# A two-layer graph attention kernel: a new order table, ScalarE writes the last outputs first, x is added by accumulating transfers

## The chip, the cores and the metric

One core of a Trainium2 chip. The metric is the device time of one execution in microseconds (us). TensorE is called PE (matmul) and PEld (its weight loads), VectorE DVE, ScalarE ACT, GpSimd POOL and SyncE SP. SP and POOL issue the transfers (DMA).

## The reference

For each of 32 graphs of 512 nodes, with x of 512 numbers a node and an adjacency matrix of integers, all in float32: a layer norm and relu, two attention layers over the graph's edges, and x added at the end.

```python
def gat_layer(x, mask, W, a_src, a_dst, bias, concat):
    xl = (x @ W).reshape(B, N, H, F)
    asrc = jnp.einsum('bnhf,hf->bnh', xl, a_src)
    adst = jnp.einsum('bnhf,hf->bnh', xl, a_dst)
    e = jax.nn.leaky_relu(asrc[:, :, None, :] + adst[:, None, :, :], NEG_SLOPE)
    e = jnp.where(mask[..., None], e, NEG_INF)
    attn = jax.nn.softmax(e, axis=1)
    out = jnp.einsum('bsdh,bshf->bdhf', attn, xl)
    ...
h = jnp.maximum(_layernorm(x, axis=-1), 0.0)
h = jax.nn.elu(gat_layer(h, mask, W1, ..., concat=True))      # 4 heads of 256
x = x + gat_layer(h, mask, W2, ..., concat=False)             # 1 head of 512
```

## The kernel before, in words

Each graph goes through the same steps: `norm` (statistics on DVE, a power on POOL, the relu on ACT), `project1` (x times W1 for two pairs of heads), a softmax for each head, `gather1` (attention times projected nodes, with bias and ELU), `project2`, the softmax of the second layer, and `gather2`, which adds x and stores. Products are split into halves and done by seven products instead of eight (`sevens`); in `project1` the fifth of the seven is split once more into seven small ones of 128x129, the function `step`. A small product goes into one half of a bank `top` (keys tk+0 and tk+1) or straight into a result bank; ACT copies the result of the first, fourth and fifth out of `top` (the fifth into a buffer f), and DVE adds the sixth and seventh.

A softmax tile p of 128x512 per source block is made on DVE (`L517 ... p<-rr,z`, from normalisers rr that are spread over the partitions by a small store to DRAM and a load back, drr and rr on SP), gets the mask added by an accumulating transfer from DRAM that POOL issues (`p<-dm`, L525, two per pair of blocks), and goes through exp on ACT (`p<-p,z`). DVE sums p tiles into tiles t and hs for the seven products; PE multiplies them with xl.

`gather2` writes its result through `put`: for each of its seven products and two row blocks a result bank is scaled by the softmax share and added by DVE onto a tile t, which `residual` has loaded with x before (SP, 256 KB); when a tile t is complete SP stores it.

Nothing is emitted where it is written. Every instruction group is a job of the class `Program` (engine, cost, what it reads and writes), and `order()` decides the order in which jobs are emitted, and with it the order on each engine. Before, it is a list scheduling: a simulated clock with the costs and a model of the transfers (KIND), the job with the lowest rank first among those that are ready. The rank is a number of the table PLACES, one for each job of the start, of one turn, and of the end; the turn's numbers are used again for each graph, moved on by the turn's PE time. A turn has 470 jobs and works on the projection, the softmax and the gathers of neighbouring graphs side by side. Each engine runs its instructions in order, and waits for semaphores of others.

In the profile every operation of a helper has one line: L531 PE, L514 ACT, L517 DVE, L520 the transfers of SP, L525 those of POOL, L770 the power. Banks of PSUM are called mm, the weights w_sb, normalised and transposed x ht, sums of halves hs, hx (of activations) and wx (of weights, for the small products).

Of the kernel before, what the change touches and what calls it, by code (L numbers as in the profile page):

```python
# [19 lines left out]
P = 128  # L20
EPS = 1e-5
# [23 lines left out]
class Banks(Slots):  # L45
# [1664 lines left out]
```

## Time and profile before

| | us |
|---|---|
| time, median of 3 runs | 2773.44 |
| lowest, highest run | 2768.58, 2775.35 |
| the profiled execution | 2769.33 |
| its span | 2767.6 |

The rows of the profile that the prediction shows are read thus. A row of a timeline has the start and the length in us, the engine, the line, the operation, what is written and read, the shape, the count of instructions put together, and in brackets the time for which the engine stood before it and what ended that. A row of groups has the count, the busy time and the mean in ns of one, and the idle time before. A row of waits has who waited for whom: total, times, longest. Of an issue row the last number is the median time to landing.

### The profile page before, as it was taken

The numbers are of one execution on the slowest core, as the hardware profiler recorded it, in microseconds if no ns is written. First come the engines' busy times: TensorE is split into PE (matmuls) and PEld (weight loads), VectorE is DVE, ScalarE is ACT, GpSimd is POOL, SyncE is SP. The second block draws the span as 40 slices with busy tenths as digits, with TensorE's granted clock in tenths as the row PEclk, the third lists the DMA queues.
The fourth block names the chain that finished last, engine by engine and source line by source line (L and its number), as shares of the span: only waits on it lengthen the run. The fifth ranks groups of instructions, "written<-read, shape, count | busy, mean of one in ns | idle before, by whom it ended". The sixth has DMA issues, their size and how long they took to land. (4 is left out here: it accounts for less than half of the span.)

```text
span 2767.6 us, 42320 instructions
## 1 busy us (share of the span) xinstructions
PE 2742.4 (99%) x12924; PEld 2371.8 (86%) x12924; DVE 2558.2 (92%) x6732; ACT 2229.1 (81%) x4907; POOL 313.1 (11%) x356
## 2 busy tenths in 40 slices
PE   7999999999999999999999999999999999999999
PEld 6788888888888888888888888888888888888887
DVE  8999999999999999999999999999999999999996
ACT  5978888778887788877888877888778788788883
POOL 0110111101111111111011111111111111101110
PEclk9999999999999999999999999999999999999999
DMA  8657766667666667667676766766676767767563
GB/s 232 176 157 182 203 167 184 187 176 194 182 183 179 182 176 196 178 175 195 173 201 172 182 187 178 192 186 180 180 188 175 201 167 180 195 165 208 162 171 112
DMA packets 375864, 502.14 MB, mean 181 GB/s; under 512 B 222804, under 2 KB 227668, under 8 KB 375636
## 3 DMA queue, kind: packets, MB, share of 16 engines
q1 hardware_dynamic: 329844, 332.68, 42.4%
q0 software_dynamic: 45792, 166.74, 25.1%
q8 instruction: 103, 1.69, 0.3%
q14 instruction: 125, 1.02, 0.1%
HBM read 316.41 MB, written 51.31 MB: 133 GB/s over the span
## 5 line engine op out<-in xcount | busy, mean ns | idle before, releaser
L531 PE MATMUL mm<-w_sb,hs 128*128 128x257 f32 (+3 forms) x2908 | 667.0, 367 | 5.1 <-ACT mm L514 3.3
L531 PEld LDWEIGHTS mm<-w_sb,hs 128*128 128x128 f32 x2908 | 539.7, 190 | 87.7 <-ACT mm L514 6.7
L525 POOL DMA_DIRECT2D p<-dm x314 | 273.2, 875 | 2295.0 <-DVE p L517 764.3
L531 PE MATMUL mm<-w_sb,ht 128*128 128x258 f32 x2112 | 528.6, 382 | 2.7 <-ACT mm L514 2.5
L531 PE MATMUL mm<-p,xl 128*128 128x258 f32 (+1 forms) x1984 | 495.8, 383 | 0.1
L531 PE MATMUL mm<-w_sb,h 128*128 128x257 f32 x2056 | 477.8, 379 | 0.0
L517 DVE SCALAR_TENSOR_TENSOR p<-rr,z 128x512 f32<-128x512 f32 (+1 forms) x636 | 456.0, 742 | 2.4 <-DMA rr<-drr 2.4
L531 PEld LDWEIGHTS mm<-w_sb,ht 128*128 128x128 f32 x2112 | 393.7, 190 | 63.6 <-ACT mm L514 6.4
L514 ACT ACTIVATE p<-p,z 128x512 f32<-128x512 f32 (+1 forms) x636 | 433.4, 720 | 17.7 <-DVE p L517 12.4
L531 PEld LDWEIGHTS mm<-w_sb,h 128*128 128x128 f32 x2056 | 389.0, 189 | 58.4 <-ACT xl L514 0.5
L531 PEld LDWEIGHTS mm<-p,xl 128*128 128x128 f32 x1984 | 367.2, 190 | 52.7 <-issue 6.0
L514 ACT ACTIVATE mm<-mm 128x257 f32<-128x257 f32 (+2 forms) x498 | 169.8, 347 | 269.2 <-PE mm L531 236.2
L514 ACT ACTIVATE l<-as,z 128x512 f32<-128x512 f32 x516 | 354.4, 716 | 30.8 <-DMA as<-das 30.7
L514 ACT ACTIVATE l<-l,low 128x512 f32<-128x512 f32 x516 | 370.3, 721 | 7.6 <-DVE low L517 6.7
L517 DVE CUSTOM_DVE_ANT_1 l<-l,mt 128x512 f32<-128x512 f32 x516 | 346.2, 681 | 28.4 <-ACT l L514 27.4
L514 ACT ACTIVATE xl<-mm 128x258 f32<-128x258 f32 (+2 forms) x748 | 269.3, 382 | 91.4 <-PE mm L531 89.8
L514 ACT ACTIVATE h<-mm,b_sb 128x256 f32<-128x256 f32 (+1 forms) x504 | 231.0, 480 | 77.3 <-PE mm L531 76.6
L531 PE MATMUL mm<-t,hs 128*128 128x258 f32 (+1 forms) x992 | 246.1, 380 | 0.0
L517 DVE TENSOR_TENSOR xl<-xl,mm 128x258 f32<-128x258 f32 x372 | 155.3, 419 | 57.9 <-PE mm L531 48.3
L531 PEld LDWEIGHTS mm<-t,hs 128*128 128x128 f32 x992 | 185.8, 190 | 25.5 <-DVE t L517 0.2
L531 PE MATMUL mm<-xl,p 128*128 128x258 f32 (+2 forms) x752 | 189.7, 388 | 1.0 <-ACT h L514 0.6
L517 DVE SCALAR_TENSOR_TENSOR h<-xr,h 128x512 f32<-128x512 f32 x256 | 172.2, 683 | 6.1 <-ACT xr L514 6.1
(137 smaller groups left out, 3706.2 us busy)
## 6 DMA issues: line engine op xcount, KB each, us to landing
p<-dm POOLq DMA_DIRECT2D x314, 512.0 KB, 5.0
rr<-drr SPq DMA_DIRECT2D x159, 512.0 KB
x<-in_x_dram SPq DMA_DIRECT2D x129, 256.0 KB
adj<-in_adj_dram SPq DMA_DIRECT2D x128, 256.0 KB
as<-das SPq DMA_DIRECT2D x64, 512.0 KB
t<-in_x_dram SPq DMA_DIRECT2D x124, 256.0 KB
out_dram<-t SPq DMA_DIRECT2D x124, 256.0 KB
dm<-m SPq DMA_DIRECT2D x64, 256.0 KB
```

Source lines behind the costliest of these rows:

```text
L514: prog.add("ACT", cost, reads, writes, lambda: nc.scalar.activation(*a, **k))
L517: prog.add("DVE", cost, reads, writes, lambda: f(*a, **k))
L525: lambda: nc.gpsimd.dma_start(to, at, accum_op=OP.add), size,
L531: f(*a, **k)
```

## The change

Seven edits; the costs of jobs are no times, only what the order is made from.

1. `order()` is replaced. Each engine's jobs are sorted by rank (a new PLACES, in ten-thousandths of a microsecond instead of hundredths); the five lists are then merged by the lowest rank whose inputs have been emitted. The simulated clock and the model of transfers go. The order is so the same in each turn.
2. A small product that goes into `top` is listed as writing both halves of it, so that the next one comes behind the copy of the one before.
3. In `put` of `gather2`, products 2, 5, 6 and 4 are written to t by ACT as scaled copies, and only 3 and 7 are added by DVE: in each turn 8 of 12 adds become copies.
4. `residual` loads x only for the last graph. For the others POOL issues an accumulating transfer of x onto the finished t, 256 KB, four in a turn, and the store waits for its landing.
5. The norm of the first graph goes by tiles: four powers and shifts instead of one.
6. The identity for the first transposes lies in the buffer hx of the small products, and those transposes are listed as reading it.
7. The loads of the start come in another order, by the new table.

```diff
     def order(self):
...
+        lines = {e: [] for e in self.ENGINES}
+        for j in sorted(range(len(jobs)), key=lambda j: (rank[j], j)):
+            lines[jobs[j][0]].append(j)
+        lines = [deque(q) for q in lines.values()]
+        while any(lines):
+            q = min((q for q in lines if q and not left[q[0]]), key=lambda q: rank[q[0]])
+            j = q.popleft()
             done.append(j)
...
-        every = [sk + (t,) for t in range(NT)]
...
+        for ts in ([t] for t in range(NT)) if b == 0 else [range(NT)]:
+            every = [sk + (t,) for t in ts]
...
-                akeys + bkeys + ([tk + (1,)] if q == 1 else []), [bk], w / 576,
+                akeys + bkeys, [tk + (0,), tk + (1,)] if bk[:2] == tk else [bk], w / 576,
...
-            dma(XLOAD, [x2_key(b, 0, 0)], halves, xr, x[b, d * P : (d + 1) * P, :])
+            if b == B - 1:
+                dma(XLOAD, [x2_key(b, 0, 0)], halves, xr, x[b, d * P : (d + 1) * P, :])
+            else:
+                for c in range(2):
+                    prog.alias(xk + (c,), [xk, xk + (c,)])
...
-            dve(
-                PUT, [bk, sk, xk + (c,)], [xk + (c,)], nc.vector.scalar_tensor_tensor,
-                to, ps[:, :M], share, to, op0=OP.mult, op1=OP.add,
+            if n in (3, 7):
+                dve(
+                    PUT, [bk, sk, xk + (c,)], [xk + (c,)], nc.vector.scalar_tensor_tensor,
+                    to, ps[:, :M], share, to, op0=OP.mult, op1=OP.add,
+                )
+            else:
+                act(COPY, [bk, sk, xk], [xk + (c,)], to, ps[:, :M], AF.Copy, scale=share)
...
+                halves = [xk, xk + (0,), xk + (1,)]
+                accumulate(XADD, halves, halves, xt, x[b, d * P : (d + 1) * P, :])
                 dma(STORE, [xk, xk + (0,), xk + (1,)], (), out[b, d * P : (d + 1) * P, :], xt)
```

What the new order does at three places. First ACT in a turn, at the small products of the first pair of heads: `mm<-mm 128x129` is the copy of the first small product, `f<-mm` that of the fifth, `p<-p,z` are the exps. Before:

```order
L514 ACTIVATE mm_137<-mm_139 128x258
L514 ACTIVATE p_103<-p_103,z_127 128x512 x2
L514 ACTIVATE h_82<-mm_134,b_sb 128x256
L514 ACTIVATE xr_96<-h_82 128x512
L514 ACTIVATE p_103<-p_103,z_127 128x512 x2
L514 ACTIVATE mm_135<-mm_132 128x129
L514 ACTIVATE f_92<-mm_132 128x129
```

And of the change:

```order
L469 ACTIVATE mm_136<-mm_138 128x258
L469 ACTIVATE p_102<-p_102,z_126 128x512 x2
L469 ACTIVATE f_91<-mm_131 128x129
L469 ACTIVATE h_75<-mm_132,b_sb 128x256
L469 ACTIVATE p_102<-p_102,z_126 128x512
L469 ACTIVATE mm_134<-mm_131 128x129
L469 ACTIVATE xl<-mm_138 128x258
L469 ACTIVATE p_102<-p_102,z_126 128x512
```

Both copies stood behind four exps; now f stands behind two and the other behind three.

On PE at the same place (each matmul listed here shows as two in the profile, so that x2 is the profile's x4, and one of 128x129 is a whole small product). Before:

```order
L531 MATMUL mm_132<-wx_85,hx_86 128x129
L531 MATMUL mm_132<-w_sb,hs 128x129
L531 MATMUL mm_136<-p_104,xl 128x256 x2
L531 MATMUL mm_133<-w_sb,hs 128x129
L531 MATMUL mm_132<-wx_85,hx_86 128x129
L531 MATMUL mm_139<-w_sb,ht 128x258 x2
```

And of the change:

```order
L486 MATMUL mm_131<-wx_78,hx_79 128x129
L486 MATMUL mm_138<-w_sb,hs 128x258 x2
L486 MATMUL mm_131<-w_sb,hs 128x129
L486 MATMUL mm_134<-p_101,xl 128x256 x2
L486 MATMUL mm_132<-w_sb,hs 128x129
L486 MATMUL mm_131<-wx_78,hx_79 128x129
L486 MATMUL mm_138<-w_sb,ht 128x258 x2
```

Between the two products into the bank `top`, which followed each other, there now stands a large one.

Third POOL, from one power of the norm to the next. Before:

```order
L770 TENSOR_TENSOR stats_124<-stats_124,half 128x4
L525 DMA p_104<-dm_120 128x1024 x2
L525 DMA p_102<-dm_120 128x1024 x2
L525 DMA p_103<-dm_122 128x1024 x2
L525 DMA p_104<-dm_121 128x1024 x2
L525 DMA p_102<-dm_121 128x1024 x2
L770 TENSOR_TENSOR stats_123<-stats_123,half 128x4
```

And of the change:

```order
L480 DMA p_103<-dm_120 128x1024 x2
L480 DMA p_101<-dm_119 128x1024 x2
L480 DMA t_108<-in_x_dram 128x512
L480 DMA t_106<-in_x_dram 128x512
L480 DMA t_105<-in_x_dram 128x512
L728 TENSOR_TENSOR stats_123<-stats_123,half 128x4
L480 DMA p_102<-dm_119 128x1024
L480 DMA t_107<-in_x_dram 128x512
L480 DMA p_102<-dm_119 128x1024
```

The last pair of mask adds of a turn, which stood ahead of the power, now stands behind it and behind three and four of the transfers of x.

More of the change, by code (lines that the diff above doesn't have):

```diff
@@ L2 @@
 from contextlib import ExitStack
-from heapq import heappop, heappush
 import concourse.bass as bass
@@ L286, in ranks @@
         turn = sum(job[1] for job in self.jobs[first : first + each] if job[0] == "PE")
-        rank, self.place = [], []
         for j in range(n):
             if j < first:
-                v, i = j, 0
+                yield PLACES[j] / 10000
             elif j < last:
-                v, i = first + (j - first) % each, (j - first) // each + 1
+                yield PLACES[first + (j - first) % each] / 10000 + turn * ((j - first) // each + 1)
             else:
-                v, i = first + each + j - last, (last - first) // each + 1
-            self.place.append(v)
-            rank.append(PLACES[v] / 100 + turn * i)
-        return rank
+                yield PLACES[first + each + j - last] / 10000 + turn * ((last - first) // each + 1)
     def order(self):
-        jobs, rank = self.jobs, self.ranks()
-        n = len(jobs)
-        after = [[] for _ in range(n)]
+        jobs, rank, done = self.jobs, list(self.ranks()), []
+        after, left = [[] for _ in jobs], [len(job[2]) for job in jobs]
         for j, job in enumerate(jobs):
@@ L305, in order @@
                 after[d].append(j)
-        left = [len(job[2]) for job in jobs]
-        ready_at, self.start, done = [0.0] * n, [0.0] * n, []
-        free, soon, ready = dict.fromkeys(self.ENGINES, 0.0), defaultdict(list), defaultdict(list)
-        wires, now, behind = {"SP": deque(), "POOL": deque()}, 0.0, {"SP": 0.0, "POOL": 0.0}
-        for j in range(n):
-            if not left[j]:
-                heappush(soon[jobs[j][0]], (0.0, j))
-        def release(j, at):
-            for s in after[j]:
-                ready_at[s] = max(ready_at[s], at(s))
-                left[s] -= 1
-                if not left[s]:
-                    heappush(soon[jobs[s][0]], (ready_at[s], s))
@@ L321, in step @@
-        def step(until):
-            nonlocal now
-            busy = [q for q in wires if wires[q] and wires[q][0][1] <= now]
-            speed = dict.fromkeys(wires, 1.0)
-            if len(busy) == 2:
-                speed["SP"], speed["POOL"] = self.kind(wires["SP"][0][0])[2:]
-            event, which = until, None
-            for q in wires:
-                if wires[q]:
-                    j, since, todo = wires[q][0]
-                    t = now + todo / speed[q] if q in busy else since
-                    if t < event:
-                        event, which = t, q
-            for q in busy:
-                wires[q][0][2] -= (event - now) * speed[q]
-                behind[q] -= (event - now) * speed[q]
-            now = event
-            if which in busy:
-                j = wires[which].popleft()[0]
-                release(j, lambda s: event + self.kind(j)[1] + LATE.get(self.place[j], 0) / 100)
-            return which is not None
@@ L344, in order @@
-        while len(done) < n:
-            t, e = float("inf"), None
-            for q in self.ENGINES:
-                if ready[q]:
-                    at = free[q]
-                elif soon[q]:
-                    at = max(free[q], soon[q][0][0])
-                else:
-                    continue
-                if q in wires:
-                    at = max(at, now + behind[q] - self.AHEAD)
-                if max(at, now) < t:
-                    t, e = max(at, now), q
-            if step(t):
-                continue
-            while soon[e] and soon[e][0][0] <= t:
-                k = heappop(soon[e])[1]
-                heappush(ready[e], (rank[k], k))
-            j = heappop(ready[e])[1]
-            self.start[j] = t
-            free[e] = t + jobs[j][1]
-            done.append(j)
-            if jobs[j][4] is not None:
-                wires[e].append([j, free[e] + self.kind(j)[0], jobs[j][4]])
-                behind[e] += jobs[j][4]
-            else:
-                release(j, lambda s: t + jobs[j][1] + self.latency(j, s))
+        lines = {e: [] for e in self.ENGINES}
@@ L371, in order @@
+        for j in sorted(range(len(jobs)), key=lambda j: (rank[j], j)):
[4 more added lines that the diff above has]
+            j = q.popleft()
+            done.append(j)
+            for k in after[j]:
+                left[k] -= 1
         return done
@@ L443, in tile_gat @@
     nc.scalar.preload_act_table_set("natural_log_exp_and_others")
-    identf = sbuf.tile([P, P], F32, name="identf")
-    make_identity(nc, identf)
-    diag = sbuf.tile([P, P], BF16, name="diag")
-    nc.vector.tensor_scalar(diag, identf, -1.0, BIG, op0=OP.add, op1=OP.mult)
     half = sbuf.tile([P, NT], F32, name="half")
@@ L468, in tile_gat @@
     hx = {n: sbuf.tile([P, 3, P], F32, name=f"hx{n}") for n in SMALL}
+    identf = hx[SMALL[0]][:, 0, :]
+    make_identity(nc, identf)
+    diag = sbuf.tile([P, P], BF16, name="diag")
+    nc.vector.tensor_scalar(diag, identf, -1.0, BIG, op0=OP.add, op1=OP.mult)
     rs = sbuf.tile([P, 2, 2, 2], F32, name="rs")
@@ L557, in tile_gat @@
     ROWS = {4: 1.09, 8: 2.23}
+    XADD = 1.9
     COPY, ADD, TINY = 0.266, 0.335, 0.08
```

50 lines of the change are left out of this document (13 added, 37 removed), and 349 rows, old and new, of the table PLACES.

## The prediction, made before the result was known

> **What bounds the kernel now.** I read the first part of the page, then the stretches, then the groups. The page's busy times, each with its share of the span:
>
> ```profile
> span 2767.6 us, 42320 instructions
> PE 2742.4 (99%) x12924; PEld 2371.8 (86%) x12924; DVE 2558.2 (92%) x6732; ACT 2229.1 (81%) x4907; POOL 313.1 (11%) x356
> ```
>
> TensorE is the bound: 99% busy. The three other shares matter only where one of them makes TensorE wait. A busy PE isn't yet a PE at its peak, so next comes its pitch, from the timeline of PE in an undisturbed piece (start, length, engine, line, matmul, count):
>
> ```profile
> 1011.07 2.77 PE L531 MATMUL mm<-w_sb,ht 128*128 128x258 f32 x12
> 1013.68 1.03 PE L531 MATMUL mm<-t,hs 128*128 128x256 f32 x4
> ```
>
> Twelve products start in 1013.68 − 1011.07 = 2.61 us, 0.2175 us each. No edit changes the number or the width of the matmuls, so only time in which PE stands still can be won. Where is it? The stretches by engine (start and end; busy time of PE, PEld, DVE, ACT and POOL; clock, DMA share, GB/s), and the starts of four turns on PE:
>
> ```profile
> 12.00:56.00 44.00, 41.45 (x192) 35.51 (x193) 38.94 (x162) 24.95 (x57) 1.12 (x1) 0.96 0.96 274
> 216.00:2515.00 2299.00, 2294.14 (x10916) 2001.33 (x10915) 2150.37 (x5593) 1888.56 (x4160) 263.58 (x297) 1.00 0.69 183
> 2515.00:2763.00 248.00, 246.79 (x1130) 207.99 (x1129) 215.66 (x548) 174.07 (x388) 23.67 (x27) 1.00 0.58 160
> ```
>
> ```profile
> 215.93 1.03 PE L531 MATMUL mm<-p,xl 128*128 128x258 f32 x4
> 642.98 1.03 PE L531 MATMUL mm<-p,xl 128*128 128x258 f32 x4
> 727.66 1.03 PE L531 MATMUL mm<-p,xl 128*128 128x258 f32 x4
> 2515.38 1.03 PE L531 MATMUL mm<-p,xl 128*128 128x258 f32 x4
> ```
>
> From 215.93 to 2515.38 lie 27 turns, 2299.45 us, 85.16 each. The turn that begins at 642.98 lasts 84.68. Were all like it, the 27 would take 2286.4: **13.1 us is about all that the turns can give back**. Ahead of them are 12 us of lead-in and about 2.6 us of standing in the stretch 12 to 56; behind them 1.2 us, and an end after the last matmul. The table of waits (total, times, longest) says what PE stood for:
>
> ```profile
> PE mm L531 <- ACT x L514: 12.1, 1, 12.1
> PE mm L531 <- ACT mm L514: 5.8, 10, 1.2
> PEld mm L531 <- ACT mm L514: 13.6, 22, 1.6
> ACT p L514 <- DMA p<-dm: 5.2, 8, 1.4
> ```
>
> Apart from the first normalised x, it is ScalarE's copies within PSUM. One case shows why (timelines of POOL, ACT and PE):
>
> ```profile
> 992.88 0.86 POOL L525 DMA_DIRECT2D p<-dm  x1 [2.38 <-PE mm L531]
> 1000.46 1.33 ACT L514 ACTIVATE p<-p,z 128x512 f32<-128x512 f32 x2 [1.37 <-DMA p<-dm]
> 1001.70 0.26 ACT L514 ACTIVATE mm<-mm 128x129 f32<-128x129 f32 x1
> 1002.01 0.49 PE L531 MATMUL mm<-w_sb,hs 128*128 128x129 f32 x2 [1.18 <-ACT mm L514]
> ```
>
> The mask add issued at 992.88 landed near 1000.4; ScalarE stood 1.37 us before two exps of its tile; the small product's copy is queued behind those exps; PE stood 1.18 us for the copy. So the loss in the turns is a late transfer passed on by ScalarE's order.
>
> **The change, part by part.** Sums go against the profiled run, 2769.3 us (span 2767.6 and 1.7 around it); the median of the runs is 2773.4, and the profiled run lies near their lower end.
>
> *Order at the small products.* Now the copy f of the fifth small product stands ahead of the second pair of exps, and the copy of the first between the two exps of that pair. A tile that lands 1.4 us late no longer holds both copies; it holds one. PE sees more distance too: two products of four matmuls each (4 x 0.2175 = 0.87) lie between the fifth and the second instead of one. Listing them as writing the whole bank costs PE nothing itself; it only forbids q1 directly behind q5. I expect most waits of this kind to go, some to come back at the second copy: half of 13.1, so **−6**, between −13 (every turn like the shortest) and +15 (rival A).
>
> *Last output on ScalarE.* Groups by form (busy, mean ns):
>
> ```profile
> L517 DVE SCALAR_TENSOR_TENSOR t<-mm,rs,t 128x256 f32<-128x256 f32 x360 | 165.6, 474 | 8.9 <-PE mm L531 7.6
> L514 ACT ACTIVATE xl<-mm 128x257 f32<-128x257 f32 x248 | 90.8, 379 | 16.1 <-PE mm L531 16.0
> ```
>
> Of twelve adds in a turn eight become copies on ACT: DVE gives 8 x 0.47 = 3.8 us, ACT takes 8 x 0.38 = 3.0. In the turns ACT is busy 1888.56 of 2299, 82%; it goes to 86%, DVE from 94% to 89%. Neither becomes the bound on the mean, and the bank that a put frees is needed again only after several products, so by itself **0**. What it costs is ScalarE's free time just where it must answer quickly (rival A).
>
> *x by accumulating transfers.* Groups, issues and the queue's share for the nearest operation, the mask add:
>
> ```profile
> L525 POOL DMA_DIRECT2D p<-dm x314 | 273.2, 875 | 2295.0 <-DVE p L517 764.3
> p<-dm POOLq DMA_DIRECT2D x314, 512.0 KB, 5.0
> t<-in_x_dram SPq DMA_DIRECT2D x124, 256.0 KB
> q0 software_dynamic: 45792, 166.74, 25.1%
> ```
>
> POOL issues four more in a turn, 4 x 0.875 = 3.5 us, on an engine busy 263.58 of 2299. For the 16 DMA engines, 25.1% of 2767.6 over 318 adds (314, and 4 into another tile) is 2.18 us for a mask add of 512 KB. An x-add has half its bytes and takes the place of a load of the same 256 KB: net between 0 and 2.18 each, 0 to 8.7 us in a turn of 85, which lifts the share of 0.69 to 0.79 at most. I take the lower half, as the load goes away, and it hides behind PE. What it can delay is queued behind it (timelines of POOL, SP and ACT, same turn):
>
> ```profile
> 715.12 0.86 POOL L525 DMA_DIRECT2D p<-dm  x1 [1.99 <-DVE p L517]
> 725.71 0.51 SPq L520 DMA_DIRECT2D rr<-drr  x1
> 728.43 0.74 ACT L514 ACTIVATE p<-p,z 128x512 f32<-128x512 f32 x1
> ```
>
> The last mask add of a turn is issued at 715.12, 72.1 into it. Now four x-adds and the power are ahead; I place it at 74 to 75. Before, it landed near 715.12 + 0.86 + 5.0 = 721, and its exp ran at 728.43: 7.4 us of cover against 2 to 3. On SP the stores now wait for the landing, some 5 us, and the fourth stands ahead of a load of the spread normalisers. Its x-add is issued near 73, so the store goes near 79, and that load went at 725.71, 82.7 into the turn. Cover about 4 us: **0**, up to rival B.
>
> [...]
>
> *First norm by tiles.* The start, by engine:
>
> ```profile
> 9.31 1.04 POOL L770 TENSOR_TENSOR stats<-stats,half 128x4 f32<-128x4 f32 x1 [8.00 <-DVE stats L517]
> 11.20 2.23 ACT L514 ACTIVATE x<-x,stats 128x512 f32<-128x512 f32 x3 [9.16 <-DVE stats L517]
> 12.06 2.82 PE L531 MATMUL mm<-identf,x 128*128 128x128 f32 x12 [12.06 <-ACT x L514]
> 13.21 0.43 DVE L517 SCALAR_TENSOR_TENSOR xr<-w_sb,p 128x256 f32<-128x256 f32 x1 [1.30 <-DMA p<-in_L_gnn_att_dst_dram]
> 14.67 1.57 PE L531 MATMUL mm<-w_sb,ht 128*128 128x258 f32 x4
> ```
>
> One power for four tiles waits for the fourth; four powers let the first tile go earlier: by hand its transposes begin near 9.5 instead of 12.06. But now all four transposes stand ahead of the first weight product, the last shift on DVE is queued behind score rows that wait for att_dst (landed 13.2), and ScalarE's copies wait for the fourth norm. I place that product at 14.9 to 15.1 (14.67 before), 0.3 later, but with the fourth tile's transposes done, which came among the products before: at the pace of the first twelve (14.67 − 12.06 = 2.61) four are 0.87. Three more powers of 1.04 stand on an idle POOL. Net **−0.5**, from −1.5 to +1. In the 2.6 us of the stretch 12 to 56 the new order may win or lose: **−1**, from −2.6 to +3.
>
> *The end.* VectorE's last wait but for PE's own results:
>
> ```profile
> 2753.33 0.88 DVE L517 SCALAR_TENSOR_TENSOR p<-rr,z 128x256 f32<-128x256 f32 x2 [1.16 <-DMA rr<-drr]
> ```
>
> It stood 1.16 us for normalisers on their way through DRAM. Now stores that wait for x-adds stand ahead of those loads on SP, so it may come 1.5 us later, with a few products as cover: **+1**, from −1 to +3.
>
> Sum: 2769.3 − 6 + 0 + 0 − 0.5 − 1 + 1 = **2762.8, forecast 2763 us**. All lows together give 2769.3 − 13 − 1.5 − 2.6 − 1 = 2751.
>
> **Rivals.**
>
> A, slower: ScalarE answers too late at the small products. The new order is the same in each turn, so a stall, where one is, comes 31 times. From the end of the fifth product to the second are 0.87 + 0.22 + 0.87 = 1.96 us of PE (0.22: the two matmuls of half the width in between); ScalarE has in it the copy f (0.26), a bias copy, an exp (1.33 / 2 = 0.67) and the second copy (0.26), about 1.6 with the bias copy taken as the 0.38 of the row above. It decides once ScalarE comes over 0.4 us late to the first of these. For it speaks ScalarE's 3.0 us more in each turn; against it that the copies are out from behind one pair of exps. Price 0.4 to 1 us a turn, 12 to 31 us: about 2782 to 2800, middle 2790. Chance 0.16.
>
> B, slower: the queues. If x-adds take a whole mask add's 2.18 us, the last mask add or the fourth store lands over 4 us later than I think and ScalarE waits for DMA each turn, as in the case at 1000.46: 1.2 us x 31 = 37, at half the turns 18: about 2785 to 2806. Against it speak the 4 to 7 us of cover. Chance 0.08.
>
> C, nothing: late transfers simply stall elsewhere, since each waiting engine is in order; the 13.1 us of the turns stay and the edges cancel: 2769, from 2766 to 2777. Only 0.5% of the time stands still in the turns, which speaks for it. Chance 0.28. That the new order doesn't do what it says can be read from it and isn't a case.
>
> **How the numbers follow.** Forecast 0.48 (2751 to 2767), C 0.28, A 0.16, B 0.08. The range 2750 to 2790 holds the forecast, C and half of A, and leaves out some 0.15. About 0.3%, 8.3 us, is what a measurement of this kernel can tell from no change: faster means under 2765.1, slower over 2781.8. Faster is nine tenths of the forecast and a bit of C, 0.46; slower A and B nearly whole, 0.22; within, 0.32.
>
> **What would show it.** Right: turns near 84.8 us, the same one after another; "PEld mm <- ACT mm" well under 13.6; no PE wait for ACT p or DMA; DVE busy 2558 − 31 x 3.8 = 2440 and ACT 2229 + 31 x 3.0 = 2322. A: the same PE wait at a 128x129 product in every turn. B: long waits "ACT p <- DMA p<-dm", landing over 5.0. C: turns scattered around 85.2 as before. The start is wrong if the first weight product comes after 15.5. I would be wrong altogether if DMA times, not the engines' orders, set the turn's 84.68.

## The result and the profile after

The changed kernel takes **2777.59 us** (median of 20 runs, 2774.24 to 2782.3) against 2769.02 of the kernel before in the same jobs (20 runs, 2765.89 to 2775.35): ratio 1.0029, 95% interval 1.0022 to 1.0035. It is slower, by a little; the forecast was faster, 2763. The profiled execution took 2775.5 us. Of e9_all below the profiled execution took 5917 us, over twice its four other runs, so that this run has a ratio and no pieces.

The page of the changed kernel, the lines on the span and the engines:

```profile
span 2773.7 us, 42781 instructions
PE 2744.5 (99%) x12924; PEld 2377.7 (86%) x12924; DVE 2484.4 (90%) x6490; ACT 2322.4 (84%) x5155; POOL 448.7 (16%) x483
```

TensorE still does the same 12924 matmuls and is the bound; the work that moved from DVE to ACT and to POOL shows in their busy times. The same stretches as before (start and end; busy time of PE, PEld, DVE, ACT, POOL; clock, DMA share, GB/s):

```profile
12.00:56.00 44.00, 39.92 (x192) 33.28 (x191) 38.35 (x155) 23.64 (x55) 1.02 (x1) 1.00 0.86 254
216.00:2515.00 2299.00, 2298.46 (x10940) 2012.49 (x10939) 2087.99 (x5386) 1976.31 (x4386) 385.16 (x407) 1.00 0.74 183
2515.00:2763.00 248.00, 244.30 (x1118) 205.84 (x1117) 208.06 (x524) 184.12 (x413) 35.11 (x39) 1.00 0.61 153
```

In the stretch of the turns PE now stands only 2299 − 2298.46 = 0.5 us (4.9 before), so the turns did get better. It is what lies ahead of them and behind them that lost. The first and the last turn's first product on PE say by how much:

```profile
221.58 0.60 PE L486 MATMUL mm<-p,xl 128*128 128x258 f32 x2
2516.71 1.03 PE L486 MATMUL mm<-p,xl 128*128 128x258 f32 x4
```

| us | before | after | difference | forecast |
|---|---|---|---|---|
| to the first turn | 215.93 | 221.58 | +5.65 | −1.5 |
| 27 turns | 2299.45 | 2295.13 | −4.3 | −6 |
| last turn and end | 252.2 | 257.0 | +4.8 | +1 |
| span | 2767.6 | 2773.7 | +6.1 | −6.5 |

The pieces don't hold quite the same work. Counted on PE, the 27 turns have 10916 matmuls before and 10924 after, the last turn 1096 and 1088: eight matmuls `mm<-w_sb,h` now come in the first turn instead of the last, 8 x 0.2175 = 1.7 us. For equal work the turns won 6.0 us, and the last turn and the end lost 6.5.

The table of waits of the changed kernel (who for whom: total, times, longest):

```profile
PEld mm L486 <- ACT mm L469: 6.5, 17, 1.4
DVE t L472 <- DMA t<-in_x_dram: 5.2, 1, 5.2
PE mm L486 <- DVE xl L472: 4.0, 2, 3.5
ACT p L469 <- DMA p<-dm: 2.8, 5, 0.8
DVE p L472 <- DMA rr<-drr: 2.5, 2, 2.3
PE mm L486 <- ACT mm L469: 1.7, 3, 1.0
```

The waits for ScalarE's copies, 13.6 and 5.8 before, fell to 6.5 and 1.7, as hoped. Two single waits are new: PE for `xl` of DVE, 3.5 us once, and DVE for the x of the last graph, 5.2 us once. One row of before, on which the prediction says nothing, has no counterpart any more:

```profile
ACT l L514 <- DMA as<-das: 30.7, 33, 2.3
```

These are ScalarE's waits for the spread scores `as`, which go through DRAM as the normalisers do; 29.0 us of them, in 31 waits, lay in the turns.

**The one long stand of PE** is ahead of the first turn. Timelines of PE and DVE there:

```profile
180.70 1.03 PE L486 MATMUL mm<-w_sb,hs 128*128 128x258 f32 x4
184.47 0.69 DVE L472 TENSOR_TENSOR xl<-xl 128x512 f32<-128x512 f32 x1
185.21 2.09 PE L486 MATMUL mm<-xl,p 128*128 128x258 f32 x4 [3.48 <-DVE xl L472]
187.09 2.62 PE L486 MATMUL mm<-w_sb,ht 128*128 128x258 f32 x8
189.55 1.03 PE L486 MATMUL mm<-x,hs 128*128 128x258 f32 x4
```

PE is ready for the product `mm<-xl,p` at 181.73 and waits 3.48 us for a sum `xl<-xl` that DVE does last of all. The twelve matmuls after it take 189.55 − 185.21 = 4.34 us instead of 12 x 0.2175 = 2.61: 1.73 us more. So the place costs 5.2 of the 5.65 us. The stretches in two-us steps show why the second part is lost (same columns, clock third from the end):

```profile
185.00:187.00 2.00, 1.79 (x4) 1.51 (x5) 0.16 (x1) 0.00 (x0) 0.00 (x0) 0.53 0.00 0
187.00:189.00 2.00, 2.00 (x7) 1.57 (x6) 0.00 (x0) 0.49 (x2) 0.00 (x0) 0.62 0.00 0
```

The granted clock was 0.53 and 0.62 there, and 1.00 from 181 to 185 and from 189 on; in half-us steps it was 0.50 from 185.5 to 188.5. Not every execution shows this: in e17 below PE stood 3.49 us at the same product, and the clock stayed at 1.00, so that the twelve matmuls took 191.72 − 189.00 = 2.72 us; and before the change it fell to 0.50 behind a stand of 1.32 us, the longest of that kernel behind its start:

```profile
189.00 1.14 PE L486 MATMUL mm<-xl,p 128*128 128x258 f32 x4 [3.49 <-DVE xl L472]
189.00:191.00 2.00, 2.00 (x9) 1.77 (x10) 0.00 (x0) 0.37 (x1) 0.00 (x0) 1.00 0.00 0
```

```profile
49.40 1.65 PE L531 MATMUL mm<-w_sb,hs 128*128 128x258 f32 x4 [1.32 <-DVE hs L517]
50.00:53.00 3.00, 3.00 (x11) 2.54 (x10) 2.94 (x10) 1.96 (x6) 0.00 (x0) 0.50 0.83 190
```

The 1.73 us are so what this execution lost, not a fixed price of the stand.

**The end** of the changed kernel, from the last 32 products on (PE, POOL, DVE, SP):

```profile
2752.84 0.86 POOL L480 DMA_DIRECT2D mt<-in_x_dram  x1 [9.30 <-ACT mt L469]
2753.05 0.38 SPq L475 DMA_DIRECT2D rr<-drr  x1
2753.93 14.01 PE L486 MATMUL mm<-xl,p 128*128 128x512 f32 x32 [0.96 <-ACT p L469]
2758.05 0.48 DVE L472 SCALAR_TENSOR_TENSOR p<-rr,z 128x256 f32<-128x256 f32 x1 [2.32 <-DMA rr<-drr]
2759.75 1.90 SPq L475 DMA_DIRECT2D t<-in_x_dram  x4
2766.37 2.48 DVE L472 TENSOR_TENSOR t<-mm,t 128x512 f32<-128x512 f32 x4 [5.18 <-DMA t<-in_x_dram]
2769.00 1.19 SPq L475 DMA_DIRECT2D out_dram<-t  x2
```

From the first of the 32 products to the end of the span are 2773.7 − 2753.93 = 19.8 us, against 2767.6 − 2749.97 = 17.6 before. The x of the last graph is loaded at 2759.75, behind a store that waits for its x-add, and DVE stands 5.18 us for it. PE isn't held by this: its 32 products run through in 14.01 us (13.9 before), and the last add ends 0.9 us behind them (0.7 before). But the four adds, and with them the stores, now come all at once: from the last add's end to the end of the span are 2773.7 − 2768.85 = 4.85 us, against 3.0 before. That is 1.9 of the 2.2 us.

### The profile page after: what moved, and what is told of

Read it like the earlier page. It is cut to its first block, busy times and chain, and to the rows that moved or that the text cites. A ratio compares the mean times of both kernels' runs of the same rounds, so it can differ in the third digit from the quotient of the medians.

```text
span 2773.7 us, 42781 instructions
## 1 busy us (share of the span) xinstructions
PE 2744.5 (99%) x12924; PEld 2377.7 (86%) x12924; DVE 2484.4 (90%) x6490; ACT 2322.4 (84%) x5155; POOL 448.7 (16%) x483
## 3 DMA queue, kind: packets, MB, share of 16 engines
q1 hardware_dynamic: 311988, 300.17, 39.5%
q0 software_dynamic: 63648, 199.26, 32.5%
q14 instruction: 126, 1.03, 0.1%
## 5 line engine op out<-in xcount | busy, mean ns | idle before, releaser
L480 POOL DMA_DIRECT2D p<-dm x314 | 283.7, 905 | 2071.3 <-DVE p L472 853.2
L486 PE MATMUL mm<-w_sb,ht 128*128 128x258 f32 x2112 | 522.4, 382 | 1.0 <-ACT mm L469 1.0
L486 PE MATMUL mm<-p,xl 128*128 128x258 f32 (+1 forms) x1984 | 513.1, 384 | 1.0 <-DVE h L472 0.5
L469 ACT ACTIVATE xl<-mm 128x258 f32<-128x258 f32 (+2 forms) x748 | 261.0, 378 | 63.8 <-PE mm L486 57.1
L472 DVE TENSOR_TENSOR xl<-xl,mm 128x258 f32<-128x258 f32 x372 | 142.0, 414 | 32.4 <-PE mm L486 30.1
```

The costliest lines, as they stand in the source:

```text
L469: prog.add("ACT", cost, reads, writes, lambda: nc.scalar.activation(*a, **k))
L472: prog.add("DVE", cost, reads, writes, lambda: f(*a, **k))
L480: lambda: nc.gpsimd.dma_start(to, at, accum_op=OP.add), size,
L486: f(*a, **k)
```

## The experiments

The pieces of every run, read from the timelines of PE as above (us; "last turn" is from its first product to the first of the last 32). The ratio is to the kernel before in the same job, with its 95% interval.

| run | first turn at | mean of 27 turns | last turn | the rest | ratio |
|---|---|---|---|---|---|
| before | 215.93 | 85.16 | 234.6 | 17.6 | |
| changed | 221.58 | 85.00 | 237.2 | 19.8 | 1.0029 (1.0022–1.0035) |
| e1_sum_early | 216.29 | 85.00 | 235.6 | 19.6 | 1.0009 (1.0001–1.0018) |
| e2_narrow | 215.54 | 84.95 | 236.9 | 19.8 | 1.0010 (1.0001–1.0018) |
| e3_xload_first | 224.22 | 84.94 | 236.9 | 19.7 | 1.0032 (1.0019–1.0044) |
| e4_no_xadd | 221.67 | 85.05 | 237.2 | 18.0 | 1.0034 (1.0021–1.0048) |
| e7_listing | 221.90 | 84.95 | 236.5 | 19.7 | 1.0030 (1.0019–1.0042) |
| e10_exp_first | 222.58 | 85.53 | 236.0 | 19.8 | 1.0083 (1.0070–1.0097) |
| e13_exp_first_old_listing | 222.06 | 85.53 | 237.0 | 19.7 | 1.0095 (1.0079–1.0110) |
| e12_start | 215.91 | 84.98 | 235.6 | 19.8 | 1.0011 (1.0002–1.0020) |
| e15_tail | 216.23 | 85.11 | 237.2 | 18.1 | 1.0005 (0.9996–1.0014) |
| e11_turn_end | 218.71 | 85.22 | 237.0 | 22.9 | 1.0062 (1.0050–1.0075) |
| e14_turn_tail | 217.49 | 85.25 | 237.7 | 18.1 | 1.0024 (1.0014–1.0035) |
| e16_puts_dve | 225.55 | 86.48 | 239.4 | 18.0 | 1.0192 (1.0178–1.0206) |
| e17_norm_whole | 223.76 | 85.07 | 235.8 | 19.6 | 1.0040 (1.0026–1.0053) |

One profile is one execution, so the pieces scatter: where the start and the way to the first turn are the changed kernel's own, the first turn came between 221.58 and 224.22 (in the run at 224.22, e3, sixteen matmuls behind the stand took 193.11 − 186.47 = 6.64 us instead of 16 x 0.2175 = 3.48, 3.16 us lost where the changed kernel lost 1.73), and the last turn took 235.6 to 237.2. Differences below that are not read. The order on PE is the changed kernel's in all runs but the first, so their pieces hold equal work among themselves.

### The stand ahead of the first turn

In the program this product reads the half of xl2 that is 257 wide, and the DVE sum writes the other half, so the planner sees nothing between them. But `chain` gives the first matmul of a bank WIDE = 258 columns: it reads one column too many, which belongs to the other half. The new table puts the sum last. Two edits take this away in different ways. First, the sum's rank, ahead of two ELU rows on DVE:

```diff
-rank of xl<-xl, the last sum of graph 0: 1627485
+rank of xl<-xl, the last sum of graph 0: 1588518
```

> The changed kernel with one VectorE instruction of the first graph moved: the sum xl<-xl, which ran at 184.47 us, ahead of two ELU rows at 177.27. Theory A (the 258-wide product at 185.21 reads one column of the other half, so it waits for this sum, and the sum stood last in VectorE's queue): the stand of 3.48 us goes, and with it the eight products after it at twice the pitch (1.7 us); span 2773.7 - 5 = 2768 to 2769. Rival B (ScalarE's exps hold VectorE at 180.7, so whatever stands there is late): the product then waits for something else just as long, span 2772 to 2774.

Timelines of DVE and PE with the sum early:

```profile
177.32 0.69 DVE L472 TENSOR_TENSOR xl<-xl 128x512 f32<-128x512 f32 x1
181.62 1.03 PE L486 MATMUL mm<-xl,p 128*128 128x258 f32 x4
```

The product runs at 181.62 without a wait. The first turn comes at 216.29, 5.3 us earlier, and the ratio falls from 1.0029 to 1.0009; the intervals don't meet. That DVE's order was late could still be all of it, whatever the width. So the second edit leaves the order alone and narrows that one matmul:

```diff
-            n = WIDE if start and k == 0 else width
+            n = WIDE if start and k == 0 and len(prog.jobs) != 1047 else width
```

> The changed kernel with no instruction moved: the first matmul of that one product reads 257 columns instead of 258, so that it no longer touches the half which the late sum writes. Theory A: the same gain as from moving the sum, span 2768 to 2769, and the sum still ends near 185.2. Rival B: no change, 2772 to 2774, with the product waiting for another operand.

Timelines of PE and DVE with the narrow matmul:

```profile
180.88 1.03 PE L486 MATMUL mm<-xl,p 128*128 128x257 f32 x4
183.80 0.68 DVE L472 TENSOR_TENSOR xl<-xl 128x512 f32<-128x512 f32 x1
```

Now the product runs 2.9 us *ahead* of the sum it waited for. The wait was for one column that the product doesn't need: the two runs show it.

### The order of copies and exps in the turns

Theory A says that the copies f and mm, moved out from behind the exps, made the turns shorter. Its undoing, in all turns: all four exps of the tile ahead of the two copies, as before the change.

```diff
-ranks of the third and fourth exp: 1401531, 1428386
+ranks of the third and fourth exp: 1401483, 1401484 (ahead of both copies)
```

> The changed kernel with one thing of the turn put back: in each turn all four exps of the first pair of blocks stand ahead of the copies f and mm of the small products, as in the kernel before. Theory A (the turns got shorter because these copies no longer stand behind exps that wait for a mask add): the 27 turns, 2295.1 us in the changed kernel, get 3 to 10 us longer, with waits of PE for ACT f and ACT mm again. Rival B (the gain of the turns comes from elsewhere: the order being the same in each turn, VectorE's lighter load, or earlier transfers): the turns stay within 1.5 us.

The waits, and PE in one turn, of that run:

```profile
PEld mm L486 <- ACT f L469: 22.6, 29, 1.0
PE mm L486 <- ACT f L469: 11.1, 29, 0.6
```

```profile
1009.68 0.49 PE L486 MATMUL mm<-w_sb,hs 128*128 128x129 f32 x2 [0.37 <-ACT f L469]
```

29 waits, one in nearly every turn, at exactly the small product; the turns grow from 85.00 to 85.53, 14 us in all where Theory A had 3 to 10, and the ratio to 1.0083. So the new table needs the copies ahead: with the rest of it new, the old order of ACT costs more than in the kernel before. It isn't the loss of before that comes back, though. There a turn lost time now and then, when a transfer was late; here every turn loses the same 0.5 us, and ScalarE waits only 2.1 us in all for mask adds. How much of the gain the copies' new place gave is not shown by this.

The other part of that edit, listing small products as writing both halves of a bank, was undone alone, and then together with the exps:

```diff
-                akeys + bkeys, [tk + (0,), tk + (1,)] if bk[:2] == tk else [bk], w / 576,
+                akeys + bkeys + ([tk + (1,)] if q == 1 else []), [bk], w / 576,
```

> The changed kernel with the small products listed as before (only the half that they write, and the first one also reading the other half): the order on all engines stays as it is, only waits fall away. Theory A (the listing costs PE nothing by itself, since a large product stands between): total and turns within 2 us of the changed kernel. Rival B (the listing makes PE wait for the copy f in each turn): the turns get shorter by 3 us or more.

> The run with all four exps ahead of the copies, with the small products listed as before as well, so that no product waits for the copy f of the fifth any more. Theory A (the wait of 0.5 us in each turn of that run was the new listing's: the next product into the bank waits for f): the turns come back to 84.8 to 85.2 and the total to 2774 +- 3. Rival B (the copy of the first product is late as well and holds the second): turns of 85.2 to 85.5, PE waiting for ACT mm in place of ACT f.

Alone it gives 1.0030 and turns of 84.95: no difference. Together with the exps the waits for f stay (23.7 in 29 waits, 85.53 a turn): the theory that they hang on the listing fell, and the rival's wait for `mm` in place of `f` didn't come either. By itself the listing neither costs nor gains.

### The puts on ScalarE

The eight scaled copies of a turn alone go back to DVE, each placed in DVE's order where it could run in the changed kernel:

```diff
-                act(COPY, [bk, sk, xk], [xk + (c,)], to, ps[:, :M], AF.Copy, scale=share)
+                dve(COPY, [bk, sk, xk], [xk + (c,)], nc.vector.tensor_scalar_mul, to, ps[:, :M], share)
```

> The eight writes of the last output that the change gave to ScalarE in each turn are VectorE's again, placed in VectorE's order where their data were ready in the changed kernel; all else as in the changed kernel. Theory A (the puts cost and bring nothing by themselves, the copies' order alone made the turns shorter): VectorE near 2484 + 248 x 0.47 = 2600 us busy, ScalarE near 2322 - 248 x 0.38 = 2228; turns of 84.8 to 85.2 on the mean (85.00 in the changed kernel), span 2772 to 2778 (2773.7 there). Theory B (the time that VectorE gained by the puts is what lets it answer the small adds early enough): turns over 85.3, waits of PE for DVE at the small products in every turn, span over 2782.

Theory A fell. Theory B's times came (turns of 86.48, 1.5 us more each, ratio 1.0192), but its reason didn't: no small product waits for DVE in every turn. The waits of the turns and of what lies around them (216 to 2560) of this run, and the one row of it for the changed kernel:

```profile
ACT mm L469 <- DVE t L472: 183.2, 108, 2.4
PEld mm L486 <- DVE t L472: 20.7, 56, 0.4
PEld mm L486 <- ACT xl L469: 18.3, 27, 0.8
```

```profile
ACT mm L469 <- DVE t L472: 75.2, 54, 1.7
```

And one case of this run (DVE, ACT, PE):

```profile
1067.33 0.48 DVE L472 SCALAR_TENSOR_TENSOR t<-mm,rs,t 128x256 f32<-128x256 f32 x1
1067.84 0.39 ACT L469 ACTIVATE mm<-b_sb 128x257 f32<-128x257 f32 x1 [2.37 <-DVE t L472]
1068.91 0.92 PE L486 MATMUL mm<-x,p 128*128 128x256 f32 x3
```

What waits is the bank. A put empties it, then ACT writes a bias into it, and PE's next product goes in. On DVE a put takes its turn among tiles of 0.7 and 1.2 us and comes late; ACT stands for it, and PE waits in each turn twice for a put and once for ACT's `xl`. On ACT the put that empties and the copy that refills are on one engine. So the puts are part of what the shorter turns need, with this order; with the order of before, DVE did them in time (PEld waited for its `t` twice, 0.6 us in all), and the price found here is that of one placement, not the least that could be had.

### x by accumulating transfers

The accumulating transfers become nothing, so that for 31 of the 32 graphs x is not added to the output:

```diff
-                accumulate(XADD, halves, halves, xt, x[b, d * P : (d + 1) * P, :])
+                prog.add("POOL", 0.95, halves, halves, lambda: None, XADD)
```

> The changed kernel with the accumulating transfers of x left out, so that the output lacks x for all graphs but the last; the order on all engines stays. Theory A (the transfers are hidden in the turns and cost only at the end): the 27 turns stay at 85.0 us on average (2295 +- 2 us), and the end gets 2 to 3 us shorter, since nothing waits for a landing there. Rival B (they lengthen the turns by contention and by POOL's queue): the turns get shorter too, by 3 us or more over the 27.

POOL's queue in the changed kernel, then without the x-adds (packets, MB, share of the 16 DMA engines):

```profile
q0 software_dynamic: 63648, 199.26, 32.5%
```

```profile
q0 software_dynamic: 45792, 166.74, 24.7%
```

124 x-adds take 0.325 x 2773.7 − 0.247 x 2773.1 = 216 us of the queue, 1.75 us each. Against the kernel before the loads that fell away go off: SP's queue went from 42.4% of the span to 39.5%, and POOL's from 25.1% to 32.5%, which leaves about 1.0 us each. In the turns that is hidden: their mean is 85.05 without them and 85.00 with them. At the end it isn't: the rest is 18.0 instead of 19.8 (17.6 before), though a ratio can't tell so little (1.0034 against 1.0029). Does the end lose by the store that stands ahead of the last loads of x? Those loads were put ahead of it on SP:

```diff
-ranks of the four loads of x of the last graph: 2761070, 2759255, 2764233, 2766738
+ranks of the four loads of x of the last graph: 2748590 to 2748593
```

> The changed kernel with the four loads of x of the last graph ahead of the store of mt on SP, behind which they stood at 2759.75. Theory A (that store waits for the landing of its accumulating transfer, and the loads queued behind it land at 2766.4, 5.18 us after VectorE wanted them): the loads go near 2755, VectorE no longer waits, and the span gets 2 us shorter (2771.5). Rival B (the transfer engines are full at the end, with the four accumulating transfers and the spread loads): the loads land as late as before, span unchanged within 0.7 us.

SP and DVE in that run:

```profile
2754.03 2.73 SPq L475 DMA_DIRECT2D t<-in_x_dram  x4
2765.57 0.69 DVE L472 TENSOR_TENSOR t<-mm,t 128x512 f32<-128x512 f32 x1 [2.93 <-DMA t<-in_x_dram]
```

Issued 5.7 us earlier than in the changed kernel, the loads still held DVE until 2765.57, and the rest stayed at 19.7. Theory A (order on SP) fell. Rival B fits, that the transfers themselves are crowded: x-adds of the graph before, stores, a load of normalisers and four loads of x lie within some 10 us, and in the changed kernel the DMA share is 1.03 from 2756 to 2760 and 0.84 from 2760 to 2768, where before it was 0.39 from 2753 to 2757 and 0.30 from 2757 to 2764.

Then the last graph but one was handled as before the change (loads near 2690, adds on DVE, no x-adds in the last 30 us), together with the early sum and the start of e12 below:

```diff
-            if b == B - 1:
+            if b >= B - 2:
...
-            if n in (3, 7):
+            if n in (3, 7) or b == B - 2:
...
+                if b < B - 2:
```

> The changed kernel with the early sum of the first run, the mended start, and for graph 30 alone the handling of x put back to that of the kernel before: four loads on SP near 2690 and adds on VectorE, no accumulating transfers in the last 30 us. Theory A (those transfers crowd the loads of spread normalisers and of the last x in the end): the last four adds wait for PE alone, the spread load of 2753 lands in 3 to 4 us instead of 5.0, and from the start of the last 32 products to the end of the span are 17.5 to 18.2 us instead of 19.8; span 2765.8 - 1.8 = 2764. Rival B (the end is set by when the last softmax starts, which the order of PE sets): 19 us or more remain, or PE waits longer before the last 32; span 2765 to 2767.

PE and DVE of that run:

```profile
2751.31 14.01 PE L486 MATMUL mm<-xl,p 128*128 128x512 f32 x32 [0.65 <-ACT p L469]
2754.42 0.49 DVE L472 SCALAR_TENSOR_TENSOR p<-rr,z 128x256 f32<-128x256 f32 x1 [1.26 <-DMA rr<-drr]
```

The wait for normalisers falls from 2.32 to 1.26 and the rest to 18.1, inside Theory A's 17.5 to 18.2; but DVE still stands 2.67 us for the x of the last graph, and the span is 2769.4 and not 2764. This is the best version: 1.0005 (0.9996 to 1.0014), level with the kernel before and not ahead of it; against e1 and e12 the intervals overlap. Two things keep the end from being settled. Last turn and rest together are 255.3 in e15 and 255.2 in e4, but 255.2 to 257.0 in runs with x-adds. And e16, with its x-adds, also has a rest of 18.0: its loads of x were issued 4.5 us behind the first of the last 32 products and held DVE until 10.0 us behind it, against 5.8 and 12.4 in the changed kernel. The rest goes with the time at which these loads land, and the x-adds are one thing that can delay them.

### The start

One load of the start and its user go later, and the fourth tile's shift goes ahead of a score row, together with the early sum:

```diff
-ranks of one load of the start, its user, the fourth tile's shift: -4189864, -975560, -975235
+ranks of one load of the start, its user, the fourth tile's shift: -3803340, -917686, -975250
```

> The changed kernel with the early sum of the first run and the start alone (b1 loaded and used later, the shift of the fourth tile ahead of a score row). Theory A (the turn made the run with four orders slow): first weight product at 14.8 to 15.6, first turn at 215.5 to 216.3, span 2766 or a little less. Rival B (the start made it slow, by PE at half its pitch for longer or by a late bias): first turn 10 us or more later than 216.

The first weight product on PE, in the changed kernel, and then with this edit:

```profile
15.60 4.60 PE L486 MATMUL mm<-w_sb,ht 128*128 128x258 f32 x20
```

```profile
14.25 6.08 PE L486 MATMUL mm<-w_sb,ht 128*128 128x258 f32 x22
```

The first weight product comes 1.35 us earlier than in the changed kernel's profile. But with that kernel's own start it came anywhere from 14.62 (e2) to 15.78 (e16), and with this edit at 14.67 in e15; the first turn, 215.91 against 216.29 in e1, and the ratio, 1.0011 against 1.0009, show no gain. Then the norm alone, all four tiles at once again:

```diff
-        for ts in ([t] for t in range(NT)) if b == 0 else [range(NT)]:
+        for ts in [range(NT)]:
```

> The norm of the first graph is done for four tiles at once again, as before the change; all else as in the changed kernel. Theory A (the norm by tiles brings the first transposes forward and the first weight product gains nothing from it): first matmul near 12.1 us (11.18 in the changed kernel), first weight product within 0.7 of the changed kernel's 15.60, first turn within 0.7 of its 221.58, span within 1.5 of 2773.7. Theory B (the norm by tiles, with its small operations queued ahead of others, is what made the start late): first weight product at 14.9 or earlier, first turn earlier than 220.8, span under 2772.5.

PE at the start of that run:

```profile
13.64 3.34 PE L486 MATMUL mm<-hx,x 128*128 128x128 f32 x16 [13.64 <-ACT x L469]
16.82 3.43 PE L486 MATMUL mm<-w_sb,ht 128*128 128x258 f32 x15
```

Neither theory held: the first matmul came at 13.64 instead of near 12.1, and the first weight product at 16.82, 1.0 us later than in any run with the norm by tiles. The first turn, 223.76, is within the scatter, but in this execution the clock stayed up behind the stand, and the twelve matmuls took 1.6 us less than in the changed kernel's. So the norm by tiles is not what made the start late; in the new order of DVE and POOL it helps there. The ratio, 1.0040 against 1.0029, is too close to tell.

### Trying for more in the turns

In each turn about 0.12 us are lost at one large product, for a DVE sum `p<-p`. Three runs moved that sum ahead of other rows of DVE: first with all the other edits, at the start and the end too, then with the early sum and earlier loads at the end, then on top of e15 directly ahead of a small add.

```diff
-rank of the sum p<-p: 1475385
+rank of the sum p<-p: 1407941 (e9, e11), 1407944 (e14)
```

> Four orders mended together, each to be read at its own place. (1) The early sum of the first run: first turn near 216 instead of 221.6. (2) In each turn VectorE makes the sum p<-p, for which the 258-wide product p,xl stood 0.1 us, ahead of three rows that are wanted later: turns of 84.68 to 84.70 instead of 84.79, 27 x 0.1 = 3 us over all. (3) At the start b1 is loaded and used later and the shift of the fourth tile goes ahead of a score row that waits for att_dst: first weight product at 14.8 to 15.1 instead of 15.60 if the loads set it, 15.6 if VectorE's score rows do. (4) At the end two loads of x go near 2750 instead of 2759.75, away from the accumulating transfers: if the transfers' crowding is what costs the 2 us at the end, 1 to 2 us come back; if it is the order of the queue alone, it was tried already and gives nothing. Sum: 2773.7 - 6 - 3 - 0.5 - 1 = 2763, below both kernels; a rival in which new waits take the gain: 2766 to 2768.

> The changed kernel with the early sum of the first run, the earlier loads of x at the end, and the turn's sum p<-p ahead as in the run with four orders, but with the ELU row behind the second small add instead of ahead of it, so that this add, wanted by PE within 0.5 us, comes no later than 1260.1. Theory A (what made the run with four orders 20 us slow is the turn: the small add came 0.34 us late, 28 to 31 times): turns of 84.7, first turn at 216, end 1 to 2 us shorter: span 2762 to 2764. Rival B (what made it slow is the start): the turns are as fast as in A here too, and the start is told by the run next to this one.

> The same, and in each turn the sum p<-p directly ahead of the small add instead of behind it, with the ELU row moved behind the second small add. Theory A (the product p,xl 128x258 stands 0.13 us in each turn for this sum): turns of 84.68 to 84.72 instead of 84.79, 2 to 3 us less in all, span 2761 to 2762, 0.1% under the kernel before. Rival B (VectorE's queue passes the time on to the next small add, as in the two tries before): turns of 84.8 to 85.1.

e9 gave 1.0083 (1.0069 to 1.0096). e11 gave 1.0062 (1.0050 to 1.0075), e14 1.0024. The waits of e11:

```profile
PEld mm L486 <- DVE mm L472: 14.9, 31, 0.7
```

31 waits, one in each turn, for the next small add `mm<-mm,f`, which the moved sum now holds up; most turns took 85.07 instead of 84.79. In e14 the same row stands with the same numbers. DVE's queue has no slack at this place: what spares one product 0.12 us costs another about 0.4, as the turn grew by 85.07 − 84.79 = 0.28. In e11, with the loads of x earlier, DVE also stood 6.78 us for normalisers at the end, and PE 3.02 us in the middle of its last products.

## Why the prediction was wrong

**The step that failed** is one that the sum doesn't have. "Order at the small products" was worked out for the turns; the same new table orders the 160 us between the stretch 12 to 56 and the first turn, and nothing was set against them. There the product at 185.21 stood for one column that it doesn't need, 3.48 us, and lost 1.73 more at the lower clock: +5.2 (e1 and e2 show it). The order of instructions could have told it beforehand, by DVE's last sum and PE's product of 258 columns; I read the order only where the trace of before had waits. With that stand out, e1 comes to 1.0009: still no gain. The rest of the miss is the end, +1 in the sum and +6.5 for equal work: of the 12.6 us between the forecast and the measured span, 7.1 lie ahead of the first turn, 5.5 behind the turns, and none in them.

**Turns −6**: −4.3 on the clock, −6.0 for equal work, so the size was met. (The 13.1 counted the first turn like the others, but it has 412 matmuls against 404: 11.4 could be given back.) The turns became alike, as forecast: 21 of the 27 lie between 84.77 and 84.81. Nearly all of the scattered loss came back, and about 0.1 us a turn over 84.68 was newly lost. But only half of the mechanism was seen. It was read from one case; in the turns of before PE stood eight times for ScalarE, 4.4 us. Four of these stands, 2.4 us, follow an exp that waited for a mask add, as in the case shown. The four others, 2.0 us, follow ScalarE's wait for the scores `as`:

```profile
852.53 1.95 ACT L514 ACTIVATE l<-as,z 128x512 f32<-128x512 f32 x3 [2.27 <-DMA as<-das]
854.38 0.52 ACT L514 ACTIVATE mm<-mm 128x129 f32<-128x129 f32 x2
854.69 1.14 PE L531 MATMUL mm<-w_sb,ht 128*128 128x258 f32 x4 [0.81 <-ACT mm L514]
```

In the turns of the changed kernel PE has no such stand left; ScalarE doesn't wait for `as` there at all, and 1.2 us for mask adds (5.2 before). So two things changed at once: the transfers kept ScalarE waiting less, and the copies stand elsewhere; no run takes them apart. Rival A had the place right: e10 makes such a stall in every turn, 0.53 us, within its 0.4 to 1. That late transfers would stall elsewhere (rival C) didn't happen in the turns.

**Last output on ScalarE, 0 by itself**: wrong as a reason. "The bank that a put frees is needed again only after several products" doesn't hold for this order: e16 shows 1.5 us a turn when it comes late. The copy is 0.47 us and not 0.38; for ACT's total the forecast 2322 was met nevertheless; DVE's is 2484, 44 over the forecast, and why is open.

**x-adds, 0**: right in the turns (e4), at about 1.0 us each net, in the lower half of 0 to 2.18 as taken; the DMA share rose to 0.74, within the 0.79 given. ACT's wait for mask adds fell (5.2 to 2.8), so rival B didn't come there.

**Start −0.5, stretch 12 to 56 −1**: the first weight product was placed at 14.9 to 15.1. The profiled run has 15.60, beyond 15.5, where I said that the step would be wrong; the other runs with the same start code have 14.62 to 15.78. PE's busy time of 39.92 against 41.45 in the stretch is no loss: both hold 192 matmuls, and before some of them ran at the lower clock (0.96 over the stretch). By 160 us PE had started 624 matmuls, 621 before. The two terms together are so about −0.4 there instead of −1.5, and that was lost again by 180 us.

**End +1**: +6.5 for equal work. The term named normalisers behind stores that wait for x-adds. That wait rose from 1.16 to 2.32, 1.2 of the 1.5 foreseen, but by luck: on SP this load (2753.05) stands ahead of the first such store (2759.33), the wait is 2.19 without any x-adds (e4), and PE ran its last products without a stand. What cost 2.2 us in the rest is the load of x that came late; e4 and e15 take back 1.8 and 1.7. The other 4.4 us lie ahead of the last 32 products. PE's longest stands there are 1.11 us at 2682.87, for a sum that DVE came to late after 1.24 us of waiting for normalisers, and 0.96 for ACT's `p` just ahead of the 32 products; before, the longest was 0.57. Runs with the same code lost 2.7 to 4.4 us there, e4, without x-adds, as much as the changed kernel, which speaks against the x-adds. Which rows of the new table make it is open: no run took it back.

## What to carry to other kernels

A table that orders every engine must be read over the whole program, the parts that run once too: one stand of 3.5 us there, with what the clock took on top, cost nearly what 27 turns gained (5.2 us against 6.0). An operand read wider than its tile is a dependency that the table of reads and writes doesn't show; narrow it, or keep its neighbour's writer early. A transfer that is free in a loop can have its price where the loop ends and nothing hides it: here the turns took 85.05 us without the x-adds and 85.00 with them, the rest 18.0 and 19.8. And where pieces of two orders are compared, count their work first: eight matmuls that changed sides made 6.0 us look like 4.3.

## What was not expected of the hardware

The clock's answer to one and the same stand was not the same. Behind 3.48 us without matmuls it was 0.50 from 185.5 to 188.5 in the changed kernel; behind 3.49 us it was 1.00 in e17, while in e3 sixteen matmuls took 6.64 us instead of 3.48. In the kernel before it was 0.50 from 50 to 53 behind a stand of 1.32, while a stand of 0.96 ahead of the last products left it at 1.00 (2752 to 2756 of the changed kernel). These runs give no length of stand that decides it. By the shares of POOL's queue (32.5% with the x-adds, 24.7% without, 25.1% before), an accumulating transfer of 256 KB held the 16 DMA engines 1.75 us, against 2.18 for a mask add of 512 KB: half the bytes for four fifths of the time.
